# Layer 3 of a four-layer graph network: softmax sums and reciprocals kept on chip, and a regrouped order of work

## The chip, the cores and the metric

The kernel runs on one core of a Trainium2 chip. A core has five engines that work side by side, each through its own list of instructions in order: TensorE (PE; its weight loads are PEld), VectorE (DVE), ScalarE (ACT), GpSimd (POOL) and SyncE (SP), which in this kernel starts DMA transfers. Operands lie in SBUF, a memory of 128 partitions; PE writes its results to PSUM, which has 8 banks, each as large as one 128x512 float32 tile. The metric is the device time of one execution in microseconds, lower is better. The kernel before took 2297.15 us (median of 3 runs, 2293.25 to 2300.82).

## The reference, cut to what matters

`x` is (32, 512, 64): 32 batches of 512 nodes with 64 features; `adj` is a 512x512 graph. Four layers follow one another, each `x = x + layer(relu(layernorm(x)))`. The change touches layer 3 alone, a graph attention with 8 heads and a second attention behind it:

```python
def gat_layer(x, graph, W, b):
    h = x @ W
    s = jnp.einsum('bnd,bmd->bnm', h, h) * graph
    s = jnp.where(s == 0.0, NEG_INF, s)
    a = jax.nn.softmax(s, axis=2)
    return jnp.einsum('bnm,bmd->bnd', a, h) + b
heads = jax.vmap(lambda W, b: gat_layer(flow_x, graph, W, b))(Wh, bh)   # 8 heads, 128 wide
H, B, N, D = heads.shape
cat = jnp.moveaxis(heads, 0, 2).reshape(B, N, H * D)
x = jax.nn.leaky_relu(cat, negative_slope=0.01)
out = gat_layer(x, graph, W_out, b_out)                                 # 1024 -> 64
return jax.nn.leaky_relu(out, negative_slope=0.01)
```

All of it is float32. For each batch and head a 512x512 matrix of scores is formed, its row maximum is subtracted, the exponential taken, and the weighted values are divided by the sums of the exponentials.

## The kernel before, in words

**Units.** Layers 0 to 2 take the first 450 us and are not touched. Layer 3 is cut into 144 units: 128 `Heads` units (one batch, two heads) and 16 `Out` units (the second attention of a pair of batches). A unit always holds two attention matrices, `k = 0, 1`, each 512x512, in `C = 4` row blocks `r` of 128 rows. The list `flow` holds the units in order. In its regular stretch nine units follow one another: the eight Heads units of two batches and one Out unit of an earlier pair, which stands behind the first unit of the second batch. The last six units are Out units.

**Steps of a unit.** `scores(r)`: PE multiplies one row block for both k into `s_ps` (two PSUM banks; two such buffers). `maxima(r)`: DVE adds the mask, writes the negated scores to `p_att` in SBUF and keeps the row maximum; the kernel relies on these matrices being symmetric in the scaled form used, so that the maximum of a row serves a column too. `spread_out` and `spread_in`: the maxima are transposed on DVE, written to DRAM by four DMAs on SP's queue, and read back broadcast to all partitions as `topb`. `shift(r)`: POOL subtracts them. `exps(r)`: ACT takes the exponential. `totals`: PE adds up the exponentials with a matrix of ones; `tot_ps` then holds four groups of 32 equal rows: for each k, the sum over the even and over the odd row blocks. `values(j)`: PE multiplies the exponentials with the features into `av`, the one buffer of `ps_v`.

**The sums before.** ACT copies `tot_ps` to `tot` (line 425). `totals_out` writes one row of each group to DRAM (four DMAs, line 430). `totals_in` reads them back spread over 128 partitions as `parts` (one DMA, line 434). `recips` adds the halves and takes the reciprocal of a 128x8 tile on DVE (lines 441 and 444) and writes it to DRAM (line 446). `recips_in` reads it back broadcast as `recb` (two DMAs, line 451). `normalize` multiplies `av` by `recb` on DVE into `o_att` (line 457).

**Behind that.** For a Heads unit, `y_pe` (line 532) multiplies `o_att` by the head's weights, `y_act` and `y_dve` (542, 550) make the leaky ReLU into `cat`. `product` (574) multiplies `cat` by `W_out` into `gT_ps`; `keep_product` copies it (581). For an Out unit, `make_v` transposes `gT`, `make_gs` scales it on POOL and reduces its smallest size on DVE (594); `y_act`, `back`, `back_dve`, `back_pool` and `store` bring its result back, add it to `x` and write it out. For coming batches, `features` (a row of 13 small ACT instructions and a DVE reduction, line 494, at the first unit of a batch), `make_hx` and `make_g` prepare operands.

**Order.** The order is written by hand (`manual_schedule`): function `period(t)` in `planned` emits the steps of several units of different age, and each engine gets them in that order. `unit(lag)` is the unit that is `lag` periods old; `now` is `unit(0)`, `ahead` is the next one. Nothing is reordered afterwards: an engine whose next instruction waits holds up all that stands behind it. Before the change `totals` of a unit runs two periods after its scores, its values three, its `y` four, and an Out unit is stored at five. `W_out` is applied in four portions, one in each period of an odd batch.

**Buffers.** `ps_m` (three PSUM banks) serves `tot_ps`, `y_ps`, `gT_ps`, `gV_ps`, `hx_ps`, `g_ps` and `back_ps` in turn; `s_ps` has two buffers of two banks, `av` one bank. `p_att` has 14 buffers, three and a half units.

Of the kernel before, what the change touches and what calls it, by code (L numbers as in the profile page):

```python
# [8 lines left out]
F32 = mybir.dt.float32  # L9
# [5 lines left out]
P = 128  # L15
# [7 lines left out]
def fast_form(  # L23
# [284 lines left out]
    ROOM = 6  # L308
# [7 lines left out]
    class Pair:  # L316
# [98 lines left out]
        def totals(self):  # L415
# [8 lines left out]
            self.tot = wk.tile([P, N], F32, name="tot", bufs=1)  # L424
            nc.scalar.copy(self.tot, ps)  # L425

        def totals_out(self):
            self.tot_row = dram.tile([Q, N], F32, name="tot_row")
            for q in range(Q):
                nc.sync.dma_start(self.tot_row[q : q + 1, :], self.tot[q * 32 : q * 32 + 1, :])  # L430

        def totals_in(self):
            self.parts = tiny.tile([P, 2, 2, C], F32, name="parts")
            nc.sync.dma_start(
                self.parts.rearrange("p k h r -> p (k h) r"),
                self.tot_row.rearrange("q (p r) -> p q r", r=C),
            )

        def recips(self):
            rec = tiny.tile([P, 2, C], F32, name="rec_flow")  # L440
            nc.vector.tensor_reduce(  # L441
                rec, self.parts.rearrange("p k h r -> p k r h"), AX.X, OP.add
            )
            nc.vector.reciprocal(rec, rec)
            self.rec_row = dram.tile([2, N], F32, name="rec_row")
            nc.sync.dma_start(self.rec_row.rearrange("k (p r) -> p k r", r=C), rec)

        def recips_in(self):
            self.recb = wk.tile([P, N], F32, name="recb", bufs=1)
            for k in range(2):  # L450
                nc.sync.dma_start(
                    self.recb[halves(k), :], self.rec_row[k : k + 1].to_broadcast([F, N])
                )
# [107 lines left out]
    class Out(Pair):  # L561
# [8 lines left out]
        def product(self, h):  # L570
            if h == 0:
                self.gps = ps_m.tile([P, N], F32, name="gT_ps", tag="m")
            for k in range(2):
                nc.tensor.matmul(  # L574
                    self.gps[halves(k), :], lhsT=wo_sb[:, h, :],
                    rhs=Heads.cat[self.b + k, h], start=(h == 0), stop=(h == H - 1),
                )

        def keep_product(self):
            self.gT = wk.tile([P, N], F32, name="gT", bufs=LATE + 1)  # L580
            nc.scalar.copy(self.gT, self.gps)
# [8 lines left out]
        def make_gs(self):  # L590
            self.gs = wk.tile([P, N], F32, name="gs")
            nc.gpsimd.tensor_tensor(self.gs, self.gT, urow, OP.mult)

            nc.vector.tensor_reduce(
                least_out[:, self.b // 2 : self.b // 2 + 1], self.gT, AX.X, OP.min,
                apply_absolute_value=True,
            )
# [72 lines left out]
    def planned(units, products):  # L670
# [7 lines left out]
        def period(t):  # L678
# [4 lines left out]
            for r in range(2):  # L683
                now.scores(r)
            unit(4).y_pe()
            unit(2).shift(2)
            unit(2).exps(2)
            unit(4).y_act()
            unit(2).shift(3)
            unit(2).exps(3)  # L690
            unit(3).totals_out()
            unit(1).spread_in()
            unit(3).totals_in()
            for r in range(2):
                now.maxima(r)
            unit(4).y_dve()
            unit(3).recips()
            unit(3).recips_in()
            unit(5).back_pool()
            ahead.make_gs()  # L700
            unit(5).store()
            for j in range(C):
                unit(3).values(j)
# [1089 lines left out]
```

## Time and profile before

| | us |
|---|---|
| median of 3 runs | 2297.15 |
| the profiled execution's own time | 2282.12 |
| its span | 2280.3 |
| PE busy | 2127.8 (93%) |
| DVE busy | 1459.5 (64%) |
| POOL busy | 1416.3 (62%) |
| ACT busy | 1215.7 (53%) |
| first and last transposition of maxima (line 386), starts | 460.0 and 2235.1 |

The profiled execution is 15.0 us shorter than the median of the runs. The 144 transpositions of line 386, one for each unit, mark the rhythm of layer 3: 1775.1 us for 143 steps, 12.41 us for a period. In a profile's list of groups a line gives the kernel's line, the engine, the operation, the tiles (out<-in) with partitions x elements, the count, then the total busy time, the mean duration of one in ns, and the engine's idle time just before, with the releaser. A timeline line gives the start, the duration, the engine, the line and what was run; in square brackets stands how long the engine had been idle and who released it. Engines overlap the tail of an instruction with the head of the next, so that starts can lie closer together than durations. `READ_ACCUMULATOR` is the short second part of a maximum.

### The profile page before, as it was taken

The page shows a single profiled execution, that of the slowest core. Times are in us where ns is not written, and L with a number is a line of the kernel's source. Part 1 is how long each engine was busy: PE and PEld are TensorE (multiplying, and loading weights), DVE is VectorE, ACT ScalarE, POOL GpSimd, SP SyncE. Part 2 cuts the span into 40 slices and gives each one's busy share as a digit, 9 for nine tenths or more (in the row PEclk, how much of TensorE's full clock was granted, in tenths as well). Part 3 has the DMA queues.
Part 4 walks back from the last instruction along what each step waited for, and adds up shares of the span by engine and source line. Part 5 has one row for each costly group of instructions (what it writes and reads, how often), then busy time and mean ns, then how long its engine had stood idle before and what let it go on. Part 6 is the DMA issues. An engine that isn't in the chain of part 4 may idle for free.

```text
span 2280.3 us, 35348 instructions
## 1 busy us (share of the span) xinstructions
PE 2127.8 (93%) x12190; PEld 854.4 (37%) x12190; DVE 1459.5 (64%) x3953; ACT 1215.7 (53%) x1944; POOL 1416.3 (62%) x665
## 2 busy tenths in 40 slices
PE   7999999979999999999999999999999999999995
PEld 4677676623333323332333232323332323333232
DVE  6799986656656565666566656565655666566662
ACT  3443442346565656565555555565555555665543
POOL 2000000067777777877777777777777777777885
PEclk9999999899999999999999999999999999999998
DMA  4000000012222222222222222222222222222222
GB/s 128 1 1 1 1 1 1 1 58 65 69 64 72 72 63 72 63 72 72 67 67 68 67 67 68 67 67 67 69 67 71 59 72 68 62 67 72 63 67 73
DMA packets 193964, 130.67 MB, mean 57 GB/s; under 512 B 150392, under 2 KB 155680, under 8 KB 193648
## 3 DMA queue, kind: packets, MB, share of 16 engines
q1 hardware_dynamic: 193264, 128.13, 21.0%
q8 instruction: 98, 1.61, 0.3%
q0 software_dynamic: 512, 0.20, 0.1%
q14 instruction: 90, 0.74, 0.1%
HBM read 120.66 MB, written 6.55 MB: 56 GB/s over the span
## 4 chain that ended last, share of the span: by engine, by line
PE 51%; DMA 25%; DVE 10%; SPq 5%; ACT 3%; issue 3%; POOL 2%; POOLq 0%; DVEq 0%; ACTq 0%
PE av L410 12%; DMA recb<-rec_row 8%; DMA parts<-tot_row 8%; PE s_ps L367 8%; PE nt_ps L840 7%; DMA rec_row<-rec_flow 6%; PE acc L932 5%; DVE p_att L379 5%; PE gT_ps L574 4%; PE tot_ps L420 3%; PE y_ps L532 3%; DMA tot_row<-tot 2%; PE g_ps L514 2%; SPq L389 2%; SPq L430 2%
## 5 line engine op out<-in xcount | busy, mean ns | idle before, releaser
L401 POOL TENSOR_TENSOR p_att<-p_att,topb 128x1024 f32<-128x1024 f32 x576 | 1344.4, 2366 | 556.6 <-DMA topb<-top_row 400.8
L379 DVE CUSTOM_DVE_ANT_0 p_att<-s_ps,flow_neg 128x512 f32<-128x512 f32 x1152 | 725.6, 686 | 287.3 <-PE s_ps L367 286.6
L404 ACT ACTIVATE p_att<-p_att 128x1024 f32<-128x1024 f32 x576 | 605.7, 1057 | 377.4 <-POOL p_att L401 374.8
L367 PE MATMUL s_ps<-hx,g 64*128 64x512 f32 x2048 | 505.2, 611 | 1.9 <-DVE top L379 1.5
L410 PE MATMUL av<-p_att,hn 128*64 128x512 f32 x2048 | 485.0, 617 | 0.0
L367 PEld LDWEIGHTS s_ps<-hx,g 64*128 64x128 f32 x2048 | 182.0, 187 | 287.9 <-issue 184.6
L420 PE MATMUL tot_ps<-p_att,ones 128*32 128x512 f32 x2304 | 277.1, 599 | 0.0
L410 PEld LDWEIGHTS av<-p_att,hn 128*64 128x64 f32 x2048 | 139.6, 141 | 330.6 <-issue 317.0
L532 PE MATMUL y_ps<-o_att,wh_sb 64*128 64x512 f32 x512 | 140.3, 623 | 94.1 <-DVE o_att L457 93.9
L457 DVE TENSOR_TENSOR o_att<-av,recb 128x512 f32<-128x512 f32 x144 | 98.3, 682 | 178.9 <-DMA recb<-rec_row 169.2
L1008 POOL TENSOR_TENSOR x<-x,bias_b 128x512 f32<-128x512 f32 x16 | 20.3, 1273 | 279.7 <-DVE hn L782 279.7
L542 ACT ACTIVATE cat<-y_ps,bh 128x512 f32<-128x512 f32 x256 | 160.9, 679 | 59.1 <-PE y_ps L532 58.6
L550 DVE SCALAR_TENSOR_TENSOR cat<-y_ps,bh,cat 128x512 f32<-128x512 f32 x256 | 179.9, 744 | 0.0
L526 ACT COPY g<-g_ps 128x512 f32<-128x512 f32 x128 | 68.7, 589 | 180.9 <-PE g_ps L514 180.9
L441 DVE TENSOR_REDUCE rec_flow<-parts 128x8 f32<-128x16 f32 x144 | 24.4, 169 | 172.4 <-DMA parts<-tot_row 171.7
L420 PEld LDWEIGHTS tot_ps<-p_att,ones 128*32 128x32 f32 x2304 | 60.1, 109 | 194.9 <-issue 149.4
L574 PE MATMUL gT_ps<-cat,wo_sb 128*64 128x512 f32 x512 | 125.4, 594 | 0.0
L932 PE MATMUL acc<-v,s 64*128 64x65 f32 x2048 | 124.2, 280 | 0.7 <-DVE s L918 0.4
L932 PEld LDWEIGHTS acc<-v,s 64*128 64x128 f32 x2048 | 121.2, 195 | 5.9 <-DVE o L948 1.2
L840 PE MATMUL nt_ps<-adj_t,hn 128*128 128x512 f32 x256 | 116.2, 597 | 0.8 <-DVE hn L804 0.8
L532 PEld LDWEIGHTS y_ps<-o_att,wh_sb 64*128 64x128 f32 x512 | 43.8, 185 | 180.7 <-DVE o_att L457 108.0
L425 ACT COPY tot<-tot_ps 128x512 f32<-128x512 f32 x144 | 82.8, 575 | 33.8 <-PE tot_ps L420 14.9
(173 smaller groups left out, 1771.6 us busy)
## 6 DMA issues: line engine op xcount, KB each, us to landing
topb<-top_row SPq DMA_DIRECT2D x144, 512.0 KB
recb<-rec_row SPq DMA_DIRECT2D x288, 128.0 KB
top_row<-top_t SPq DMA_DIRECT2D x576, 1.0 KB
tot_row<-tot SPq DMA_DIRECT2D x576, 2.0 KB
out_dram<-y SPq DMA_DIRECT2D x32, 128.0 KB
x<-in_x_dram SPq DMA_DIRECT2D x3, 1024.0 KB
parts<-tot_row SPq DMA_DIRECT2D x144, 8.0 KB
rec_row<-rec_flow SPq DMA_DIRECT2D x144, 4.0 KB
```

The source lines that it names most:

```text
L367: nc.tensor.matmul(ps[:, k], lhsT=g[halves(k), r * P : (r + 1) * P], rhs=x[halves(k), :], start=True, stop=True,)
L379: nc.vector.tensor_tensor_reduce(out=self.p[r][:, k], in0=ps[:, k], in1=flow_neg[:, r], scale=-1.0, scalar=BIG, op0=OP.add, op1=OP.min, ac ...
L401: nc.gpsimd.tensor_tensor(self.p[r], self.p[r], self.topb, OP.subtract)
L404: nc.scalar.activation(self.p[r], self.p[r], AF.Exp, scale=-1.0)
L410: nc.tensor.matmul(self.av[halves(k), :], lhsT=self.v(k, j), rhs=self.p[j][:, k], start=(j == 0), stop=(j == C - 1),)
L420: nc.tensor.matmul(ps[q : q + 32, :], lhsT=ones, rhs=self.p[j][:, k], start=(j < 2), stop=(j >= 2),)
L532: nc.tensor.matmul(ps, lhsT=wh_sb[halves(k), 2 * self.i + k, :], rhs=self.o[halves(k), :], start=True, stop=True,)
L542: nc.scalar.activation(self.cat[:, k], self.y[k], AF.Identity, bias=bh01[:, h : h + 1], scale=0.01)
L550: nc.vector.scalar_tensor_tensor(self.cat[:, k], self.y[k], bh[:, h : h + 1], self.cat[:, k], op0=OP.add, op1=OP.max,)
L574: nc.tensor.matmul(self.gps[halves(k), :], lhsT=wo_sb[:, h, :], rhs=Heads.cat[self.b + k, h], start=(h == 0), stop=(h == H - 1),)
L840: nc.tensor.matmul(p, lhsT=lhs(k), rhs=adj_t[:, k, :], start=(k == 0), stop=(k == C - 1))
L932: nc.tensor.matmul(self.acc[k][:, r], lhsT=self.s[b // 2][halves(k), b % 2, r * P : (r + 1) * P], rhs=self.v[halves(k), b], start=(b == 0) ...
```

## The change

The way of the sums through DRAM is taken out: `totals_out`, `totals_in`, `recips_in` and their eight DMAs for a unit. In place of one copy of `tot_ps`, ACT makes four copies of 32 partitions each, which put the other half's sums beside each group (`other`). DVE adds `tot_ps` and `other` as 128x512 tiles and takes the reciprocal of the whole 128x512 tile. `tot_ps` is held in PSUM until that addition.

The order of a period is rewritten. A period starts with row blocks 2 and 3 of `now` and goes on to row blocks 0 and 1 of `ahead`. The values, the reciprocal and the normalisation of a unit come in the period of its totals, and `y`, `back`, `back_pool` and `store` one period earlier than before. `spread_in` stands right behind `spread_out`. `features`, `make_hx` and `make_g` come one period earlier, so that three earlier periods run among the layers before and one period, -1, is added in front; at the end `ROOM` is one less. `W_out` of a pair of batches is applied in one period, all 16 products in a row, and the reduction of `gT` (now line 562) follows at once, ahead of `recips` on DVE.

```diff
-    ROOM = 6
+    ROOM = 5
...
-            self.tot = wk.tile([P, N], F32, name="tot", bufs=1)
-            nc.scalar.copy(self.tot, ps)
-
-        def totals_out(self):
...
-        def totals_in(self):
...
+            self.tot_ps = ps
+            self.other = wk.tile([P, N], F32, name="other")
             for q in range(Q):
+                nc.scalar.copy(
+                    self.other[q * 32 : (q + 1) * 32, :],
+                    ps[(q ^ 1) * 32 : ((q ^ 1) + 1) * 32, :],
+                )
 
         def recips(self):
-            rec = tiny.tile([P, 2, C], F32, name="rec_flow")
-            nc.vector.tensor_reduce(
-                rec, self.parts.rearrange("p k h r -> p k r h"), AX.X, OP.add
-            )
-            nc.vector.reciprocal(rec, rec)
-            self.rec_row = dram.tile([2, N], F32, name="rec_row")
-            nc.sync.dma_start(self.rec_row.rearrange("k (p r) -> p k r", r=C), rec)
-
-        def recips_in(self):
...
+            self.recb = wk.tile([P, N], F32, name="recb")
+            nc.vector.tensor_tensor(self.recb, self.tot_ps, self.other, OP.add)
+            nc.vector.reciprocal(self.recb, self.recb)
...
+        def product(self):
+            ps = ps_m.tile([P, N], F32, name="gT_ps", tag="m")
+            for h in range(H):
+                for k in range(2):
+                    nc.tensor.matmul(
+                        ps[halves(k), :], lhsT=wo_sb[:, h, :], rhs=Heads.cat[self.b + k, h],
+                        start=(h == 0), stop=(h == H - 1),
+                    )
             self.gT = wk.tile([P, N], F32, name="gT", bufs=LATE + 1)
-            nc.scalar.copy(self.gT, self.gps)
+            nc.scalar.copy(self.gT, ps)
+            nc.vector.tensor_reduce(
+                least_out[:, self.b // 2 : self.b // 2 + 1], self.gT, AX.X, OP.min,
+                apply_absolute_value=True,
+            )
...
             now, ahead = unit(0), unit(-1)
...
             for r in range(2, C):
                 now.scores(r)
+            unit(3).y_pe()
+            unit(1).shift(0)
+            unit(1).exps(0)
+            unit(3).y_act()
+            unit(1).shift(1)
+            unit(1).exps(1)
             for r in range(2, C):
                 now.maxima(r)
             now.spread_out()
+            now.spread_in()
+            for r in range(2):
+                ahead.scores(r)
+            unit(3).y_dve()
+            for r in range(2):
+                ahead.maxima(r)
+            unit(3).back()
+            unit(1).shift(2)
+            unit(1).exps(2)
+            unit(4).back_pool()
+            unit(-2).make_gs()
+            unit(4).store()
             unit(2).totals()
+            unit(1).shift(3)
+            unit(1).exps(3)
+            for j in range(C):
+                unit(2).values(j)
+            u = products.get(t)
+            if u:
+                u.product()
+            unit(2).recips()
+            unit(3).back_dve()
+            unit(2).normalize()
+            unit(1).make_v()
+            unit(-3).make_hx()
+            unit(-2).make_g()
+            unit(-4).features(0)
+            unit(-4).features(1)
...
-        for k in range(len(flow) + ROOM):
+        for k in range(-1, len(flow) + ROOM):
             flow_period(k)
```

## The prediction

> **What bounds the kernel now.** I read the waits first. TensorE (PE) loses 93.9 us in front of `y_ps`, waiting for the normalised `o_att`; VectorE (DVE) had waited for `recb` from DRAM before that. These two rows are what the change is about.
>
> ```profile
> PE y_ps L532 <- DVE o_att L457: 93.9, 69, 3.3
> DVE o_att L457 <- DMA recb<-rec_row: 169.2, 99, 3.5
> ```
>
> Then the busy time by stretch of time, here 200 us of layer 3; the columns after the stretch are PE, PEld, DVE, ACT, POOL, the granted clock and DMA. PE is busy for 94%, DVE for 60%, ACT for 58%, POOL for 77%.
>
> ```profile
> core 0: us, PE busy (x) PEld busy (x) DVE busy (x) ACT busy (x) POOL busy (x), PEclk, DMA share, GB/s
> 1500.00:1700.00 200.00, 187.96 (x933) 60.92 (x933) 120.97 (x356) 115.80 (x184) 153.62 (x70) 0.98 0.25 68
> ```
>
> Last the timeline, for what one step costs and how late its reader starts. The reader should look at distances between starts.
>
> ```profile
> 458.67 0.08 DVE L379 DVE_READ_ACCUMULATOR2_ANT top<- 128x1 f32 x1
> 458.80 2.35 PE L367 MATMUL s_ps<-hx,g 64*128 64x512 f32 x8 [0.19 <-DVE top L379]
> 460.01 0.21 DVE L386 STREAM_TRANSPOSE top_t<-top 128x32 f32<-128x32 f32 x1
> 462.73 0.36 SPq L395 DMA_DIRECT2D topb<-top_row  x1
> 466.57 18.58 POOL L401 TENSOR_TENSOR p_att<-p_att,topb 128x1024 f32<-128x1024 f32 x8 [151.45 <-DMA topb<-top_row]
> ...
> 1173.91 1.92 PE L420 MATMUL tot_ps<-p_att,ones 128*32 128x512 f32 x16
> 1175.95 0.59 ACT L425 COPY tot<-tot_ps 128x512 f32<-128x512 f32 x1 [0.52 <-PE tot_ps L420]
> 1178.67 3.65 PE L410 MATMUL av<-p_att,hn 128*64 128x512 f32 x16
> 1182.26 1.13 PE L514 MATMUL g_ps<-hx,m 64*128 64x512 f32 x4
> 1183.42 1.07 ACT L526 COPY g<-g_ps 128x512 f32<-128x512 f32 x2 [2.43 <-PE g_ps L514]
> 1188.81 0.21 ACT L478 ACTIVATE less<-mean 128x4 f32<-128x4 f32 x1
> 1191.10 0.42 DVE L494 TENSOR_REDUCE least<-hn 128x4 f32<-128x256 f32 x1 [1.44 <-ACT hn L486]
> 1345.68 1.88 PE L574 MATMUL gT_ps<-cat,wo_sb 128*64 128x512 f32 x8
> 1347.50 1.13 PE L514 MATMUL g_ps<-hx,m 64*128 64x512 f32 x4
> ```
>
> From these starts PE issues the totals in 1.86 us, the values in 3.58, four heads of `product` in 1.82, `g` in 1.0, `y` in 1.05, two row blocks of scores in 1.86, a `hx`, `gV` or `back` in 0.55. Nine periods (eight Heads units, one Out) need 9 x (3.72 + 1.86 + 3.58) + 8 x 1.05 + 4 x 1.0 + 4 x 1.82 + 4 x 0.55 = 104.3 us. They take 9 x 12.41 = 111.7. So before, PE bounds, and all that a perfect cover of its waits could save is 7.4 us in nine periods, 118 us in 16 such groups.
>
> **What is removed.** One copy on ACT (0.575 us), the 8-wide reduction and reciprocal on DVE (0.169 + 0.203), and eight of thirteen DMA issues of each unit on SP. With them PE's wait goes; what replaces it is on DVE.
>
> **The reciprocal.** The trace has no reciprocal of 128x512, but four sizes of a small one, which the groups by shape give:
>
> ```profile
> L444 DVE RECIPROCAL rec_flow<-rec_flow 128x8 f32<-128x8 f32 x144 | 29.3, 203 | 4.9
> L833 DVE RECIPROCAL rstd<-std 128x32 f32<-128x32 f32 x10 | 3.4, 344 | 0.0
> L833 DVE RECIPROCAL rstd<-std 128x24 f32<-128x24 f32 x5 | 1.5, 302 | 2.6 <-ACT std L825 2.6
> L833 DVE RECIPROCAL rstd<-std 128x16 f32<-128x16 f32 x3 | 0.7, 249 | 0.8 <-ACT std L825 0.8
> ```
>
> (344 - 203) / 24 = 5.9 ns per element, where the 128x512 multiplication of line 457 takes 682 ns in all. For 512 elements: 203 + 504 x 5.87 = 3.16 us. Bounds: 0.69 us if the slope did not hold (the other 512-wide operations), 3.5 us by the steepest step (53 ns for 8). I take 3.16, since four sizes lie on its line. The Trainium skill ("VectorE: DVE Perf Modes", Specifications and "First, the fixed hardware budget") gives 0.96 GHz and an iterated divide with a repeat count of 8; my estimate from it, 512 x 8 / 0.96 + 156 ns, is 4.4 us and would make the sum below some 180 us longer. The rows' slope, 5.9 against 8.3 ns, speaks against it.
>
> **The chain of a plain period after.** Clock zero is the start of the maxima of row block 2, right behind the `o_att` of the period before. Four maxima at 0.61 and the read end at 2.53. Only then is the second buffer of `s_ps` free, so `ahead`'s row block 1 starts at 2.60 (0.05 to 0.07 behind a read, as at 458.80) and takes 0.93. Totals 3.53 to 5.45. ACT follows 0.12 later (1175.95 against 1173.91 + 1.92). Its four copies of 32 x 512: no such row exists; I take the distance of the two `g` copies, 3 x 0.53 + 0.57 = 2.18 (bounds 4 x 0.18, the 128x4 ACT rows, if partitions counted, and 4 x 0.59), so they end at 7.75. The addition starts at 7.85 and takes 0.73 with the gap to a dependent instruction; reciprocal 8.58 to 11.78; the multiplication gives way to the next maximum 0.61 later: **12.4 us**. Every step waits for the one before, on four queues. Beside it lie the transposition, `y_dve` (1.41) and `ahead`'s maxima (2.46) on DVE, done at 6.7, so DVE idles 1.2 us; the values, `g` and the next row blocks 2 and 3 on PE, done by 11.9; `y_act` and three exponentials on ACT, before 5.2. The 8-wide operations that went were not on this chain. 143 x (12.40 - 12.41) = **-2 us**: PE's wait of before is gone, and a DVE chain of the same length is there.
>
> A second loop runs over POOL: transposition at 2.54, `topb` landed 6.6 later (460.01 to 466.57), three shifts 7.0, an exponential 1.1, then the copies: 24.1 us for two periods, 12.05 each, just hidden. On SP, `spread_in` waits behind `spread_out` for the landing; `store` behind it waits with it, and nobody needs it.
>
> **`product` at one go.** Before, portions of 1.82 us filled PE. After, once in nine periods, PE finishes the values at 8.98 and the 16 heads at 16.3 (7.28 us). The copy of `gT` on ACT ends at 17.05. The reduction of `gT` (0.634) stands on DVE ahead of `recips`, so DVE, which had been ready for the addition at 7.85, waits for all of this: addition at 17.8, reciprocal 18.5, next zero at 22.3. That is 9.9 us more than a plain period, 16 times: **+158**. Low bound 6.3 (DVE free, only PE's 7.28 counted against its slack), high 11.7 with a half clock behind the gap. `g` in the same period takes the bank of `gT`, waits for its copy, and is done by 19.
>
> **`features`.** In these periods PE's `g` ends at 10.1, its copies at 11.3; 2.29 us later (1188.81 to 1191.10) DVE may reduce, behind `normalize` and ahead of the next maxima: 13.65, next zero 14.0. +1.6, 31 times: **+50** (0.4 to 2.6 each). Before, DVE had room for that wait.
>
> **Out units.** `back` on PE (0.55) and its ACT copy (0.6) come ahead of totals and copies, `back_dve` (0.65) between reciprocal and multiplication: +1.2, 16 times, **+19** (0 to 30).
>
> **The clock.** After these gaps PE runs slower for a while, as here behind a wait of 2.0 us:
>
> ```profile
> 1164.00:1166.00 2.00, 0.29 (x2) 0.29 (x4) 1.04 (x2) 1.23 (x2) 2.00 (x2) 1.00 0.08 23
> 1166.00:1168.00 2.00, 2.00 (x6) 0.30 (x6) 2.00 (x7) 0.92 (x3) 1.50 (x1) 0.56 0.57 181
> ```
>
> From 700 to 2200 us the stretches grant 0.99, a loss of some 17 us beside 94 us of waits, 0.18 each. After, nine periods take 9 x 12.4 + 9.9 + 3.2 + 1.2 = 125.9 us, so PE waits 21.6 x 16 = 346 us: 62 us lost, of which I take half as on the chain, **+30** (0 to 80). The Trainium skill ("TensorE: Matmul & The Clock Gate", "What's actually happening") lets the gate fall back after an idle window of about 3.4 us; by that rule my longest gap, 2.5 us, costs nothing and the sum is 30 less, but the rows above show a shorter gap doing it.
>
> **The tail.** Before, the last totals copy to the last `o_att` took 12.3 us (2256.87 to 2269.19); copies, addition, reciprocal and multiplication take 6.7: **-6**. Period -1 only takes two row blocks from period 0.
>
> **Sum:** -2 + 158 + 50 + 19 + 30 - 6 = +249. The profiled execution took 2282.1, so 2531; it lies 15.0 below the median of the runs, so **2546**.
>
> **Rivals.**
> 1. Faster: the long reciprocal costs like other 512-wide operations, 0.69 us. The chain is then 9.9 us, PE bounds with 104.3 + about 2 in nine periods, 5.4 less than before: 2297 - 16 x 5.4 - 6 = **2205**. The point that decides is about 1.4 us (249 / 143 below 3.16). For it: no row is as wide. Against it: four sizes on one line. Chance 0.06.
> 2. The bursts are swallowed: the queues hold enough ready work that `product`, `features` and the clock cost little, and the chain alone remains: 2297 - 2 + 19 - 6 = 2308, or **2370** with a quarter of them. For it: before, POOL and ACT had room. Against it: a chain without slack pays nothing back. Chance 0.14.
> 3. The `topb` loop is the bound: with `topb` landing 3 us later the two periods take 27.1, 13.55 each, 1.15 x 143 = 165 on top of the forecast: **2710**. For it: POOL already waits 400.8 us for `topb`. Against it: eight other transfers are gone. Chance 0.06.
>
> The forecast has 0.74.
>
> **Range and chances.** Reciprocal 2.9 to 3.5 us: -37 to +49; product -57 to +29; features -38 to +31; clock -30 to +50; copies up to +26. Taken together about 90 either way, and rival 2 reaches 2370; 2400 to 2650 leaves out rivals 1 and 3 and the lower part of 2. Under 0.3% (7 us) this kernel's runs cannot tell a change from none. Faster 0.06, same 0.02, slower 0.92.
>
> **What the profile after would show.** Reciprocal rows of 128x512 near 3160 ns; DVE busy up by some 3.5 us a period (to about 1960 us); ACT copies of 32x512 four to a unit; no `recb` transfers; 16 periods near 22 us between transpositions of maxima, with DVE idle until ACT's `gT`; PE waiting for `o_att` at `y_ps` still, longer than before. I am wrong if the reciprocal row is near 0.7 us, or if plain periods stand near 11.6.

## The result, and the profile after

The changed kernel took 2573.67 us (median of four runs, 2570.48 to 2580.19). The kernel before took 2297.72 us beside it. The ratio is 1.1206, with a 95% interval of 1.1178 to 1.1235. The profiled execution took 2570.48 us, 288.4 us more than that of before (2282.12).

First the page of the changed kernel: busy time by engine, then the two lines of the chain that ended last.

```profile
PE 2224.6 (87%) x12190; PEld 860.1 (33%) x12190; DVE 1976.0 (77%) x3953; ACT 1469.7 (57%) x2376; POOL 1414.5 (55%) x665
...
PE 50%; DVE 30%; ACT 13%; issue 4%; DMA 1%; POOL 1%; SPq 0%; DVEq 0%; ACTq 0%; POOLq 0%
DVE recb L435 15%; PE tot_ps L420 10%; PE s_ps L367 10%; ACT other L427 9%; DVE p_att L379 8%; PE av L410 6%; PE nt_ps L813 6%; PE acc L905 5%; PE gT_ps L556 4%; DVE recb L434 3%; DVE o_att L439 3%; PE y_ps L514 2%; PE g_ps L496 1%; ACT hn L463 1%; ACT hn L468 1%
```

No engine is busy for more than 87%, and the chain passes through three of them: the reciprocal on DVE, totals and scores on PE, the copies on ACT. That is what a loop of dependent steps looks like: everybody waits in turn.

The groups of instructions (busy time and mean ns of one behind the first bar; idle time ahead of them and its cause behind the second) give the prices of the new operations:

```profile
L435 DVE RECIPROCAL recb<-recb 128x512 f32<-128x512 f32 x144 | 482.9, 3353 | 4.9
...
L427 ACT COPY other<-tot_ps 32x512 f32<-32x512 f32 x576 | 331.9, 576 | 172.3 <-PE tot_ps L420 167.1
...
L434 DVE TENSOR_TENSOR recb<-tot_ps,other 128x512 f32<-128x512 f32 x144 | 99.4, 690 | 277.8 <-ACT other L427 277.8
...
L562 DVE TENSOR_REDUCE least_out<-gT 128x1 f32<-128x512 f32 x16 | 11.0, 687 | 163.3 <-ACT gT L561 163.3
```

DVE stands idle for 277.8 us ahead of the addition, until the copies are there, and for 163.3 us ahead of sixteen reductions of `gT`. The waits (total us, how many, longest) show where PE stands: in front of `y_ps`, for `o_att`, as before the change (93.9 us then).

```profile
DVE recb L434 <- ACT other L427: 277.8, 128, 8.8
...
PE y_ps L514 <- DVE o_att L439: 180.1, 97, 6.8
...
DVE least_out L562 <- ACT gT L561: 163.3, 16, 10.2
```

One plain period in the timeline. The first column is the start in us, the second how long it took; a bracket gives the idle time before and what ended it. The period runs from the first maximum behind one `o_att` (1400.03) to that behind the next (1412.87).

```profile
1400.03 0.68 DVE L379 CUSTOM_DVE_ANT_0 p_att<-s_ps,flow_neg 128x512 f32<-128x512 f32 x1
...
1403.66 1.92 PE L420 MATMUL tot_ps<-p_att,ones 128*32 128x512 f32 x16
...
1405.71 2.34 ACT L427 COPY other<-tot_ps 32x512 f32<-32x512 f32 x4 [1.23 <-PE tot_ps L420]
...
1408.08 0.69 DVE L434 TENSOR_TENSOR recb<-tot_ps,other 128x512 f32<-128x512 f32 x1 [1.56 <-ACT other L427]
1408.81 3.35 DVE L435 RECIPROCAL recb<-recb 128x512 f32<-128x512 f32 x1
1408.95 9.31 POOL L401 TENSOR_TENSOR p_att<-p_att,topb 128x1024 f32<-128x1024 f32 x4 [3.83 <-DMA topb<-top_row]
...
1412.27 0.69 DVE L439 TENSOR_TENSOR o_att<-av,recb 128x512 f32<-128x512 f32 x1
1412.87 0.68 DVE L379 CUSTOM_DVE_ANT_0 p_att<-s_ps,flow_neg 128x512 f32<-128x512 f32 x1
1413.01 1.73 PE L514 MATMUL y_ps<-o_att,wh_sb 64*128 64x512 f32 x4 [1.92 <-DVE o_att L439]
```

The steps stand at 3.63, 5.68, 8.05, 8.78, 12.24 and 12.84 us. DVE has no other work left from 1406.5 on and waits 1.56 us for the copies; the last line shows PE 1.92 us idle for `o_att`.

Last, nine periods in a row, cut at the transpositions of the maxima (columns: the stretch and its length, busy time of PE, PEld, DVE, ACT and POOL, granted clock, DMA share, GB/s):

```profile
1339.91:1354.86 14.95, 12.74 (x60) 3.82 (x56) 11.54 (x24) 11.56 (x26) 11.53 (x7) 0.94 0.20 55
1354.86:1367.65 12.79, 11.33 (x56) 3.49 (x56) 11.11 (x22) 8.49 (x13) 7.33 (x4) 1.00 0.13 41
1367.65:1389.74 22.09, 19.24 (x88) 6.28 (x88) 11.71 (x24) 9.18 (x15) 13.44 (x7) 1.00 0.08 25
1389.74:1402.58 12.84, 10.72 (x52) 3.10 (x52) 11.20 (x22) 7.63 (x12) 6.78 (x3) 1.00 0.11 41
1402.58:1415.43 12.85, 10.93 (x53) 3.40 (x52) 11.12 (x22) 6.98 (x11) 9.02 (x5) 0.92 0.11 43
1415.43:1430.23 14.80, 12.60 (x60) 3.82 (x56) 11.54 (x23) 11.97 (x27) 11.31 (x6) 0.95 0.12 36
1430.23:1443.03 12.80, 11.77 (x60) 3.95 (x60) 11.12 (x23) 8.93 (x14) 7.64 (x4) 1.00 0.11 41
1443.03:1455.82 12.79, 10.45 (x52) 3.19 (x52) 11.12 (x23) 8.83 (x13) 8.04 (x5) 1.00 0.12 43
1455.82:1469.60 13.78, 11.52 (x57) 3.69 (x56) 10.25 (x22) 7.36 (x11) 11.54 (x7) 0.94 0.12 39
```

Five plain periods stand at 12.8 whatever PE, ACT and POOL had to do in them. 22.09 is the period with `product`, 14.95 and 14.80 are those with `features`, 13.78 is that with an Out unit's `back`. Nine take 129.7 us, where nine of before took 111.7. This pattern repeats through most of the layer.

What `product` does in the third line is seen in the timeline of that period:

```profile
1374.07 7.04 PE L556 MATMUL gT_ps<-cat,wo_sb 128*64 128x512 f32 x32
...
1381.18 0.58 ACT L561 COPY gT<-gT_ps 128x512 f32<-128x512 f32 x1 [7.04 <-PE gT_ps L556]
1381.80 0.69 DVE L562 TENSOR_REDUCE least_out<-gT 128x1 f32<-128x512 f32 x1 [10.20 <-ACT gT L561]
...
1382.40 0.68 DVE L434 TENSOR_TENSOR recb<-tot_ps,other 128x512 f32<-128x512 f32 x1
```

DVE is idle for 10.20 us, since the reduction stands in its queue ahead of the addition whose inputs had been there since 1373.1.

### The profile page after: what moved, and what is told of

Its sections match the earlier page's. It is cut to its first block, busy times and chain, and to the rows that moved or that the text cites. A ratio compares the mean times of both kernels' runs of the same rounds, so it can differ in the third digit from the quotient of the medians.

```text
span 2568.7 us, 34050 instructions
## 1 busy us (share of the span) xinstructions
PE 2224.6 (87%) x12190; PEld 860.1 (33%) x12190; DVE 1976.0 (77%) x3953; ACT 1469.7 (57%) x2376; POOL 1414.5 (55%) x665
## 4 chain that ended last, share of the span: by engine, by line
PE 50%; DVE 30%; ACT 13%; issue 4%; DMA 1%; POOL 1%; SPq 0%; DVEq 0%; ACTq 0%; POOLq 0%
DVE recb L435 15%; PE tot_ps L420 10%; PE s_ps L367 10%; ACT other L427 9%; DVE p_att L379 8%; PE av L410 6%; PE nt_ps L813 6%; PE acc L905 5%; PE gT_ps L556 4%; DVE recb L434 3%; DVE o_att L439 3%; PE y_ps L514 2%; PE g_ps L496 1%; ACT hn L463 1%; ACT hn L468 1%
## 5 line engine op out<-in xcount | busy, mean ns | idle before, releaser
L401 POOL TENSOR_TENSOR p_att<-p_att,topb 128x1024 f32<-128x1024 f32 x576 | 1343.5, 2363 | 830.6 <-DMA topb<-top_row 485.0
L404 ACT ACTIVATE p_att<-p_att 128x1024 f32<-128x1024 f32 x576 | 594.6, 1054 | 140.8 <-POOL p_att L401 136.5
L367 PE MATMUL s_ps<-hx,g 64*128 64x512 f32 x2048 | 580.3, 661 | 69.1 <-DVE top L379 58.2
L435 DVE RECIPROCAL recb<-recb 128x512 f32<-128x512 f32 x144 | 482.9, 3353 | 4.9
L410 PE MATMUL av<-p_att,hn 128*64 128x512 f32 x2048 | 467.7, 598 | 0.0
L427 ACT COPY other<-tot_ps 32x512 f32<-32x512 f32 x576 | 331.9, 576 | 172.3 <-PE tot_ps L420 167.1
L514 PE MATMUL y_ps<-o_att,wh_sb 64*128 64x512 f32 x512 | 159.0, 696 | 216.1 <-DVE o_att L439 180.1
L367 PEld LDWEIGHTS s_ps<-hx,g 64*128 64x128 f32 x2048 | 196.9, 200 | 409.6 <-DVE top L379 238.9
L434 DVE TENSOR_TENSOR recb<-tot_ps,other 128x512 f32<-128x512 f32 x144 | 99.4, 690 | 277.8 <-ACT other L427 277.8
L562 DVE TENSOR_REDUCE least_out<-gT 128x1 f32<-128x512 f32 x16 | 11.0, 687 | 163.3 <-ACT gT L561 163.3
L556 PE MATMUL gT_ps<-cat,wo_sb 128*64 128x512 f32 x512 | 112.6, 592 | 0.0
```

The source lines that it names most:

```text
L367: nc.tensor.matmul(ps[:, k], lhsT=g[halves(k), r * P : (r + 1) * P], rhs=x[halves(k), :], start=True, stop=True,)
L401: nc.gpsimd.tensor_tensor(self.p[r], self.p[r], self.topb, OP.subtract)
L404: nc.scalar.activation(self.p[r], self.p[r], AF.Exp, scale=-1.0)
L410: nc.tensor.matmul(self.av[halves(k), :], lhsT=self.v(k, j), rhs=self.p[j][:, k], start=(j == 0), stop=(j == C - 1),)
L427: nc.scalar.copy(self.other[q * 32 : (q + 1) * 32, :], ps[(q ^ 1) * 32 : ((q ^ 1) + 1) * 32, :],)
L435: nc.vector.reciprocal(self.recb, self.recb)
```

## The experiments

My theory after this: a plain period is one round of totals, copies, addition, reciprocal, `o_att`, and the next scores, with no slack; `product`, `features`, `back` and the half clock come on top, each where it delays a member of that round. Against it stand, in turn, that PE or DVE sets the periods anyway, that `product` would cost its time wherever it stands, and that the clock is a by-product. The kernel before took 2290 to 2298 us beside every run, so differences of some 7 us between runs of different sets are not read.

**Without the reciprocal.**

```diff
 def recips(self):
     nc.vector.tensor_tensor(self.recb, self.tot_ps, self.other, OP.add)
-    nc.vector.reciprocal(self.recb, self.recb)
```

> The changed kernel with the 128x512 reciprocal left out, so that it multiplies by the sums in place of dividing by them; everything else stands. Theory 1 (a serial chain over four queues sets each period, and the reciprocal is 3.35 us of it): the chain of a plain period falls from 12.8 to about 9.4 us, TensorE becomes the bound again at 104.3 us and some waits in nine periods, so about 107 in place of 129.7: 2574 - 16 x 22.7 = about 2210 us (2190 to 2270). Rival (the copies on ScalarE, or the way of the maxima through DRAM, hold the period above 12 us anyway): 2450 us or more.

It took 2297.73 us (ratio to before 1.0023, 0.9999 to 1.0048), 276 us less than the changed kernel. The round did break: plain periods fell to between 10.3 and 12.6, the period with `product` to 18.75. But the gain is some 90 us short of the theory's, and the profile says where it went:

```profile
DVE least L475 <- ACT hn L467: 99.2, 31, 3.6
...
1113.63:1127.47 13.84, 11.41 (x56) 3.74 (x56) 8.19 (x23) 11.89 (x26) 13.84 (x9) 0.95 0.20 58
```

The first line is a wait, the second a period with `features`: it still takes 13.84, because DVE now arrives 3 us early at the reduction of `hn` and waits for ACT there. A removed wait had let the next one through. A run that moves that reduction, too, tests this:

```diff
+            elif step == 2:
+                nc.vector.tensor_reduce(
+                    least[:, b * C : (b + 1) * C], Heads.hn[b], AX.X, OP.max
+                )
             else:
                 h = Heads.hn[b]
-                nc.vector.tensor_reduce(
-                    least[:, b * C : (b + 1) * C], h, AX.X, OP.max
-                )
 ...
             for r in range(2):
                 ahead.maxima(r)
+            unit(-3).features(2)
```

> The changed kernel without the reciprocal (the output is then not normalized), as in the earlier run of 2298, and with the features' reduction moved one period on. Theory (without the reciprocal it is the wait for hn that makes the two features periods 13.8 beside 10.3 to 11): they fall to about 11 to 11.5, 32 times 2.5 is -80: 2215 (2190 to 2250). Rival (ScalarE's order or the half clock keeps them long): 2280 or more.

It took 2194.26 us (ratio 0.9563, 0.9505 to 0.962). `features` periods fell from 13.83 to 11.12. So with the reciprocal out of the way this wait was the limit there. DVE's wait for ACT in front of `cat` grew in its place, from 11.0 to 84.7 us, but here it cost less than the one that went. The reciprocal's price on this path is 276 us with the other wait in place, and 399 us between the two kernels that have the reduction late (2592.97 below, and this). The same 144 instructions have no price of their own; it depends on which wait comes next.

**Product: where the reduction stands, and portions.** Three kernels, of which the third is the kernel before with all 16 products at one go; its reduction of `gT` stays in `make_gs`, behind `recips`.

```diff
# reduction behind normalize
             nc.scalar.copy(self.gT, ps)
+
+        def smallest(self):
             nc.vector.tensor_reduce(
 ...
             unit(2).normalize()
+            if u:
+                u.smallest()
```

> The changed kernel with the reduction of gT moved on VectorE's queue from ahead of the addition and reciprocal to behind the normalisation. Theory 1 (VectorE waits for TensorE's 16 products and the copy of gT, and the reciprocal comes only then): the product period ends when TensorE has got through to the next scores, at 19.3 in place of 22.1 us, 16 x 2.75 = 44 us less: 2530 us. Rival (TensorE's burst alone sets the length of these periods): no change, 2574.

```diff
# four portions, reduction back in make_gs
-            u = products.get(t)
-            if u:
-                u.product()
+            for u, h in products.get(t, ()):
+                u.product(h)
+                if h == H - 1:
+                    u.keep_product()
```

> The changed kernel with W_out applied in four portions, in the period in which the two heads' cat is ready, and the reduction of gT with make_gs, as before the change. Theory 1 (TensorE has 1 to 2 us of idle time in each plain period, and the burst costs 9.3 us in one): a portion of 1.82 us fits into that idle time except where g is made in the same period (0.2 to 0.5 us over, twice in nine periods); 16 x 9.3 less 10: about 2435 us (2415 to 2470). Rival (TensorE's work bounds, wherever it stands): no more than 30 us less.

```diff
# the kernel before, all heads in one period
-            if b % 2 == 1:
-                products[len(flow) + 4] = [(out_unit, 2 * i), (out_unit, 2 * i + 1)]
+            if b % 2 == 1 and i == len(heads) - 1:
+                products[len(flow) + 4] = [(out_unit, h) for h in range(H)]
```

> The kernel before with this one part of the change: all 16 products of a pair of batches in one period, in place of four portions; the reduction of gT stays with make_gs. Theory 1 (the burst is dear only because VectorE's addition and reciprocal stand behind it): TensorE bounds and its work is the same, so little changes, 2297 + 15 us (2285 to 2340). Rival (a burst of 7.3 us costs by itself, since the other engines run dry behind it, 9 us each): 2297 + 149 = 2446.

The late reduction took 2505.74 us (1.0924, 1.0884 to 1.0964), 68 less than the changed kernel, more than the 44 expected; the period with `product` is 17.99 and PE is busy for all of it:

```profile
1347.10:1365.09 17.99, 17.93 (x88) 5.87 (x88) 11.90 (x23) 8.74 (x14) 13.51 (x7) 1.00 0.10 30
```

The portions took 2446.26 (1.0669, 1.0628 to 1.071), 127 less, 140 expected; its periods with portions stand at 12.84, and part of the gain is given back where `features` follows (16.8 in place of 14.95). In the 16.76 of its trace the portion stands on PE ahead of `g`, the copies of `g` stand on ACT ahead of the burst for `features`, and DVE waits 2.28 us for `hn`; 0.56 is such a wait in the changed kernel. In the kernel before, one go took 2332.28 (1.0158, 1.0112 to 1.0204), 42 more than before itself, where the theory had 15. So one go costs 42 us in the old order, where its reduction does not stand ahead of `recips`, and 127 in the new; about half of the 127 (68) is the place of one reduction of 0.69 us in DVE's queue. The rest goes with PE work that has nothing to hide behind: 17.9 us of it, where a plain period is 12.8.

**Totals early.** The matmuls of the totals and the four copies go ahead of `ahead`'s scores:

```diff
             unit(3).y_act()
+            unit(2).totals()
             unit(1).shift(1)
 ...
             unit(1).exps(2)
             unit(4).back_pool()
             unit(-2).make_gs()
             unit(4).store()
-            unit(2).totals()
```

> The changed kernel with the totals of unit(2), their matmuls and the four copies, moved from behind unit(1).exps(2) to right behind unit(3).y_act(), before ahead's scores; nothing left out. Theory (a plain period is the round of totals, copies, addition, reciprocal, o_att and the next y): the copies are then done some 5 us before VectorE asks for them, the addition loses its wait of 1.5 us in a plain period, and VectorE, busy 11.1 of 12.8 us, becomes what ends the period: plain about 11.45, features 13.5, W_out's add-back 11.5, the period with the product stays at 22; nine periods about 118 in place of 129.7, sixteen times 11.7 is -189: about 2385 (2330 to 2450). Rival (the round is set elsewhere, and the copies only wait beside it): less than 50 us, 2520 or more.

It took 2362.98 us (1.032, 1.0254 to 1.0385): 211 us less, 189 expected. Of 277.8 us that DVE had waited for the copies, 12.3 are left. Two periods of it:

```profile
1379.02:1390.22 11.20, 9.64 (x52) 3.19 (x52) 11.03 (x22) 8.49 (x12) 7.26 (x5) 1.00 0.16 47
1390.22:1411.79 21.57, 18.81 (x92) 6.38 (x88) 11.81 (x24) 9.17 (x14) 14.95 (x7) 1.00 0.08 26
```

This plain period is now 11.20 with DVE busy for 11.03 of it: the round is gone and DVE is the bound. This is the strongest evidence for the theory, since nothing was left out and no instruction got shorter. The move also takes the copies out from behind an exponential on ACT, but that had not held them: of 172.3 us that ACT stood idle ahead of the copies in the changed kernel, 167.1 ended with PE's totals. `product`'s period stays at 21.57, as the theory says.

**The features' reduction, moved by itself.** With the edit shown above:

> The changed kernel with only the features' reduction (least) moved from the period that computes hn to the next one, behind ahead.maxima; nothing left out. Theory (in the two features periods of nine VectorE waits for hn, which delays maxima and the next scores by 1 us and brings a stretch at half clock that delays the totals by another 1 us): features periods go from 14.8 to 13 to 13.8, 32 of them: -30 to -60, 2510 to 2540. Rival (the features' length is the 8 activations on ScalarE that stand ahead of the copies, whoever reads hn): within 10 us of 2570.

It took 2592.97 us (1.1318, 1.1248 to 1.1387): 19 more, where 30 to 60 less were expected. The periods with `features` did become shorter, from 14.8 and 14.95 to 13.9 and 13.82, but three others became longer:

```profile
1340.48:1355.65 15.17, 12.90 (x58) 4.26 (x56) 10.45 (x21) 6.71 (x10) 11.53 (x8) 0.84 0.11 35
...
1404.51:1419.71 15.20, 13.09 (x56) 3.77 (x52) 11.32 (x23) 8.48 (x13) 8.96 (x4) 0.84 0.11 35
1419.71:1433.94 14.23, 12.30 (x56) 3.63 (x52) 11.12 (x22) 7.27 (x11) 8.40 (x5) 0.86 0.12 39
```

These are `back`'s period (13.78 before), and the two behind `product` (12.84 and 12.85 before), now with a granted clock of 0.84 to 0.86 in place of 0.94, 1.00 and 0.92. DVE's wait for `hn` (19.1 us in the changed kernel) is gone, its wait for ACT in front of `cat` grew from 1.0 to 21.9 us. That costs the period behind `features` only 0.17 us (12.96, 12.79 before), and DVE waits for the copies later in that period anyway. The same move on top of totals early:

> The changed kernel with two moves and nothing left out: totals behind unit(3).y_act() and the features' reduction one period on. Theory (the combined run lost to totals early because the product in portions holds a PSUM bank, for which the totals then wait, not because of the features' reduction): 2363 less 32 times 2, 2300 (2275 to 2335). Rival (the moved features' reduction is what cost the combined run its gain, as it cost 22 us by itself): 2365 or more.

It took 2389.25 us (1.041, 1.0372 to 1.0449), 26 more than totals early alone; the rival was right. The timeline shows the wait that was moved and not removed. First totals early alone, in a period with `features`, then with the reduction moved:

```profile
1213.62 0.42 DVE L476 TENSOR_REDUCE least<-hn 128x4 f32<-128x256 f32 x1 [1.43 <-ACT hn L468]
```

```profile
1158.15 1.41 DVE L533 SCALAR_TENSOR_TENSOR cat<-y_ps,bh,cat 128x512 f32<-128x512 f32 x2 [2.10 <-ACT cat L525]
```

ACT's burst for `features` is some 3.4 us long. Where DVE no longer waits for its result, it waits a little later for ACT's part of `cat`, which is queued behind the burst. Over the whole run the two waits are of one size, the first before the move, the second after it (4.4 us before):

```profile
DVE least L476 <- ACT hn L468: 48.2, 31, 2.7
```

```profile
DVE cat L533 <- ACT cat L525: 48.8, 32, 2.3
```

Two such periods together took 24.5 before (13.31 and 11.20) and 24.5 after (11.46 and 13.08). The rest came in the period with `product` and the one behind it: 23.20 and 13.2, mostly 21.57 and 11.56 before. In one such pair, around 930 to 955 us, half clock falls on the totals, which take 3.00 and 3.58 us there and 1.92 otherwise. In my theory the features' cost was DVE's wait, to be taken away by moving the reduction; but the wait comes from ACT's queue and went on to the next instruction that needs ACT. Only without the reciprocal, where DVE had time to spare, did the move pay.

**Several at once.** Totals early, the features' reduction late, and `product` in portions:

> The changed kernel with three edits and nothing left out: totals as in the run with them early, W_out's product in four portions of two heads with its reduction back behind make_gs, and the features' reduction moved one period on, behind ahead.maxima. Theory (three waits, each with its own price, that add up): plain periods 11.45, no product period, features and add-back periods 11.5 to 13; nine periods 106 to 112, so 2570 less sixteen times 18 to 23.5, 2195 to 2285; I take 2265 since the first removed wait was partly given back by the features' periods. Rival (another wait takes the place, as it did with the reciprocal left out): 2330 or more, behind the kernel before.

It took 2415.99 us (1.0541, 1.0478 to 1.0605), so 53 more than totals early alone. The waits name a new one:

```profile
PEld tot_ps L420 <- DVE cat L533: 166.0, 48, 5.0
```

`tot_ps`, `y_ps` and `gT_ps` all come from the same pool of three PSUM buffers (tag m). In portions, `gT_ps` is held over four periods, and the early totals then wait until `cat` has read `y_ps`. In the kernels with totals early and `product` at one go this wait does not occur; with the portions alone, where the totals come late, it occurs as often and is shorter (48 waits, 49.5 us, the longest 1.5). So I take the held buffer for its cause; no run gave the pool a fourth buffer. Against the kernel with the same two moves and one go, the portions cost 27 us, although they also take the reduction of `gT` out of the way. One go, which is bad for the round, is good for the buffers. So the third combination keeps one go and takes the reduction of `gT` out of DVE's way:

> The changed kernel with three moves and nothing left out: totals behind unit(3).y_act(), the features' reduction one period on, W_out's reduction behind normalize; the product stays at one go. Theory (each removed wait keeps its price where no PSUM bank is held): from the 2363 of totals early, the product's period falls from 21.6 to the 17.9 that TensorE needs (16 times 3.7 is 59) and the features periods from 13.4 to 11.4 (32 times 2 is 64): 2240 (2215 to 2290), ahead of the kernel before. Rival (late reductions or half clock give it back, as the combined run did): 2300 or more.

It took 2296.63 us (1.0003, 0.9985 to 1.0021), level with before and 93 less than without the late reduction. It is also 119 less than the combination with portions, which differs from it in the portions and in where the reduction of `gT` went; in both it is out of the way of `recips`. That is next to the rival's 2300 and far from the theory's 2240: the features' move did not bring its 64. The last kernel drops it again:

```diff
             unit(3).y_act()
+            unit(2).totals()
 ...
-            unit(2).totals()
 ...
             unit(2).normalize()
+            if u:
+                u.smallest()
```

> The changed kernel with two moves and nothing left out: totals behind unit(3).y_act(), W_out's reduction behind normalize; the features' reduction stays where it was. Theory (moving the features' reduction only carries ScalarE's 3.6 us burst on to the next period's cat and adds half clock, 22 to 26 us in two pairs of runs): 2297 of the three moves less 10 to 26, 2270 to 2290, or from the other side 2363 of totals early less 16 times 4.1, 2298; I take 2285, level with or just ahead of the kernel before. Rival (together with the late reduction of W_out the features' move does pay, since the product's period then has no wait left): 2310 or more.

It took 2284.12 us (0.9936, 0.9909 to 0.9963): 11.5 us less than before, 290 less than the changed kernel by the place of two steps, and 12 less than with the features' move, the third pair in which that move costs time. Three periods:

```profile
1350.76:1361.96 11.20, 9.64 (x52) 3.19 (x52) 11.03 (x22) 8.50 (x12) 7.32 (x5) 1.00 0.15 47
1361.96:1379.43 17.47, 17.47 (x92) 5.89 (x88) 11.91 (x24) 8.75 (x14) 13.86 (x7) 1.00 0.11 32
1379.43:1391.28 11.85, 10.79 (x64) 3.19 (x56) 11.20 (x22) 7.97 (x11) 6.98 (x4) 1.00 0.12 45
```

PE fills the period with `product`, DVE the plain ones. Of the nine periods from 1238.67 to 1350.76 (112.1 us) PE works 105.4 and DVE 100.8, so that with this work the order alone has at most some 7 us in nine periods left to gain, 110 in all.

**The gap filled.** To size the clock, the matmuls of `now.scores(2)` and `(3)` are issued twice, so that PE has work while it waits for `o_att`:

```diff
             for r in range(2, C):
                 now.scores(r)
+            for r in range(2, C):
+                now.scores(r)
             unit(3).y_pe()
```

> The changed kernel with the matmuls of now.scores(2) and (3) issued twice, 2.0 us of TensorE at full clock in the 1.9 us in which it waits for o_att in a plain period; the second writes the same values, nothing is left out. Theory (that gap brings the half clock, and the half clock costs 1 us where it meets ahead's scores or the totals): no stretches at half clock in the steady part, features periods 13.8, W_out's add-back 12.9, y 0.1 later: 2570 less 32 and 16 and the irregular rest of some 30, plus 14: 2490 to 2550. Rival (the half clock has nothing to do with this gap, or costs nothing): 2570 to 2590; if the doubled matmuls end the period by themselves, above 2600.

It took 2537.01 us (1.1054, 1.1014 to 1.1095): 37 us less, with 288 row blocks of scores more to do. All nine periods run at full clock; the two with `features`:

```profile
1333.26:1347.09 13.83, 13.05 (x64) 4.34 (x64) 11.53 (x24) 11.38 (x26) 10.31 (x7) 1.00 0.21 59
...
1407.66:1421.50 13.84, 13.05 (x64) 4.34 (x64) 11.54 (x24) 11.39 (x26) 10.78 (x6) 1.00 0.10 38
```

From 14.95 and 14.80 to 13.83 and 13.84: half of what `features` seemed to cost in these two was the clock. The other periods moved by at most 0.2, `back`'s not at all, so its 1.0 us is not the clock.

## Why the prediction was right, and by how much each step was off

The predicted 2546 us lie 28 below the median, and the mechanism held: a DVE chain replaced PE's wait, and the bursts came on top at full price. Against the profiled executions the sum was +249 and the difference +288. The chain was tested by lifting its totals (2363 us, plain periods 11.20), the two bursts by moving the reduction and by portions. Term by term, from the period table and the runs:

| term | predicted | measured | from |
|---|---|---|---|
| plain period | -2 | +54 | (12.79 - 12.41) x 143 |
| `product` | +158 | +149 | (22.09 - 12.79) x 16 |
| `features` | +50 | +31 | (13.83 - 12.84) x 31, gap filled |
| Out, `back` | +19 | +16 | (13.78 - 12.79) x 16 |
| clock | +30 | +37 | 2573.67 - 2537.01 |
| tail | -6 | +2 | last transposition to the end: 47.1, 45.2 before |
| sum | +249 | +289 | |

That the measured terms add up to 289 is partly luck: the first and last periods of layer 3, which follow no pattern, are in none of the rows. And the sum of the prediction came as near as it did because `product`, `features` and `back` were put 31 us too high, against 56 too low for the plain period.

- **The plain period is the mis-sized term.** It was put at 12.4 and took 12.79, 12.84 in the period shown. By the clock of the prediction the totals start at 3.63 (3.53), the addition at 8.05 (7.85), the reciprocal at 8.78 (8.58), `o_att` at 12.24 (11.78). So 0.1 us is in the totals, 0.1 in the copies, 0.26 in the reciprocal and the gap behind it. The four copies follow each other at 0.585 us with no overlap (2.34, near the upper bound of 4 x 0.59), where I had taken the spacing of 128x512 copies. The reciprocal took 3353 ns and not 3160: from the 128x8 row it grows by (3353 - 203) / 504 = 6.25 ns for an element, above the slope of 5.87 of the smaller sizes. None is large, but a chain without slack multiplies each by 143.
- **The Trainium skill** ("VectorE: DVE Perf Modes", "First, the fixed hardware budget") had led to an estimate of 4.4 us for this reciprocal; the row of 3353 ns decides against it.
- **Product** was read from the order in DVE's queue, addition at 17.8 (17.3 measured, 1382.40 - 1365.1 by the same zero), and came out 9.3 and not 9.9 us longer. The late reduction and the portions confirm both halves of that.
- **Features** were put at 1.6 for the wait and the reduction behind it. They are 1.0, and another 1.0 that the period table shows is clock. Together the terms of `features` and clock were put at 80 and came to 68. That DVE's wait for `hn` could be taken away was not part of the prediction, but I believed it when I made the experiments; it moved to `cat`.
- **The clock** was near in size: 30 predicted, 37 by the filled gap. That is partly luck. The half that was taken as on the chain was a choice. And the waits alone do not set the loss: with the features' reduction moved PE waits for `o_att` about as long (184.6 us, 180.1 before), yet the mean granted clock is 0.938, 0.962 before. "TensorE: Matmul & The Clock Gate" in the Trainium skill ("What's actually happening") has the gate fall back after an idle window of some 3.4 us, which would have made this term nothing. In a plain period PE's gap is 1.92 us, and the half clock is there; the measurement decides.
- **The tail** was expected to gain 6 us from the shorter way, and that way did shorten: from the last copies to the last `o_att` it takes 6.9 us (12.3 before, 6.7 predicted). But the last three `o_att` now follow 14.0 and 13.7 us apart (10.4 and 9.3 before). PE's totals stand behind `back`, which waits for the `o_att` of the unit before, and at half clock they take 3.4 us in place of 1.92. Totals early lifts them over `back`, and its tail is 40.8 us.
- **The rivals** did not occur. The first fell with the long reciprocal. The second fell with DVE's 10.20 us of waiting in the period of `product`, which nothing swallowed. The third was POOL's loop over `topb`; POOL waits for it longer (485.0 us, 400.8 before), but `topb` lands no later: POOL begins 6.4 us behind the transposition (1402.58 to 1408.95; 6.6 before). Nor does the loop bind, since the copies wait for PE's totals (1.23 us in the period shown) and not for the exponential.
- Seen as said: DVE at 1976 us (1960 predicted), 576 copies of 32x512, sixteen periods of 22.1, PE's wait for `o_att` grown from 93.9 to 180.1.

What stays open: how much of the 16.8 with portions is clock, beside the longer wait for `hn`. No run filled the gap and moved the features' reduction at once, so that the loss of that move is put down to the clock by its granted clock alone. And the two moves together brought 290, 11 more than the 211 and 68 that each brought alone; what part of that is the clock was not measured.

## What to carry to other kernels

Replacing a transfer by compute shortens a path only if the new steps do not form a round through the queues: follow one unit from the first wait to the next same wait, through every engine, and compare that length with the busiest engine, not the sums of busy time. Where such a round exists, first look for a step that can start earlier; here starting the totals and copies earlier was worth 211 us, and moving one reduction of 0.69 us behind the work that others wait for 68 to 93. And a wait that is moved is not removed: ask which queue holds the producer, before counting its time as a gain.

## What the runs showed of the hardware

**The half clock falls on a fixed grid, and a window does not have to be idle.** In the changed kernel the stretches at half clock in the steady part are 3.41 us long, and they all start at whole multiples of 3.413 us from each other. Cut into stretches of that length at that phase, the period shown above gives this (first column behind the length is PE's busy time, the 0.50 or 1.00 is the granted clock):

```profile
1396.36:1399.78 3.42, 1.88 (x8) 0.58 (x8) 3.32 (x2) 1.06 (x1) 3.42 (x2) 1.00 0.00 0
1399.78:1403.19 3.41, 2.84 (x12) 0.93 (x12) 3.38 (x11) 1.86 (x3) 3.41 (x3) 1.00 0.00 0
...
1410.02:1413.43 3.41, 1.49 (x8) 0.49 (x6) 3.31 (x3) 1.06 (x1) 3.41 (x2) 1.00 0.00 0
1413.43:1416.85 3.42, 3.42 (x10) 1.27 (x8) 3.38 (x11) 2.08 (x3) 3.42 (x3) 0.50 0.02 3
```

The same gap of 1.92 us in front of `y_ps` lies in both halves. Where it is split by the grid so that a stretch keeps 1.88 us of PE work, the next runs at full clock; where a stretch has 1.49, the next runs at half. With the features' reduction moved by itself, all 62 stretches at full clock that were followed by half clock had at most 1.50 us of PE work, and all 432 others at full clock at least 1.55; in the changed kernel the same bound misses 11 of 525, so it is not sharp. With the gap filled, one of 553 had under 2.3 (1.17), and only that one was followed by half clock. The Trainium skill ("TensorE: Matmul & The Clock Gate", "What's actually happening") gives the window's length, 4096 cycles at 1.2 GHz or 3413 ns, free-running, and the stretches agree with it; its idle window does not agree, since less than 1.5 us of work in 3.41 was enough here.

This fits the move of the features' reduction, which cost time. Nine periods of the changed kernel are 129.7 us, 38 windows; with the move they are 133.1, 39 windows. In both the pattern therefore meets the grid at the same places again and again, but at other places, and a period that is 0.9 us shorter changed which gaps fall into one window. With the gap filled, where no half clock is left in the steady part, nine take some 127.85 us, 37.5 windows. That the periods settle on a whole number of windows where there is half clock was seen, but not tried on purpose.

**A copy of 32 partitions cost as much as one of 128.** 32x512 takes 576 ns on ACT, as long as the 128x512 copy of before (0.59 us), and four follow each other without overlap, 0.585 us apart.
